# First attention of a four-part layer chain: q and k of a head from one product, their lines transposed once, rows moved between partitions by on-chip transfers

## The chip, the core and the metric

The kernel runs on one core of one Trainium2 chip. Its engines are PE (matrix products, with weight loads shown apart as PEld), DVE (vector), ACT (scalar, activations), POOL (general) and SP, which only issues transfers here. The metric is the device time of one execution in microseconds (us). Three runs of the kernel before took 2008.51, 2015.03 and 2027.37 us; the median is 2015.03.

## The reference, cut to what matters

A chain of four parts works on x of shape 8 x 512 x 256 (batch, token, feature). The change touches only the first, an attention with 16 heads of 16 features, whose logits get a bias from six-component lines:

```python
q, k, v = split((x @ w_qkv.T + b_qkv))                 # 16 heads of 16
std_logits = einsum('bhqd,bhkd->bhqk', q, k) * dh ** -0.5
write_lines = exterior(x_prev @ w1_write.T, x @ w2_write.T)   # 6 numbers per token and head, unit length
read_lines = exterior(x @ w1_read.T, x @ w2_read.T)
incidence = einsum('bqhp,bkhp->bhqk', read_lines, write_lines @ J6)
weights = sigmoid(decay_logits)[h] ** (q_pos - k_pos)  # for keys before the query, else 0
logits = std_logits + incidence * weights * bias_scale # masked above the diagonal
out = softmax(logits) @ v
```

`x` here is the output of a conditioning layer (itself a small attention), `J6` reverses the six components with two signs, and `x_prev` is x one token earlier. A mixture of experts, a second attention and a quantised product follow.

## The kernel before, in words

`stage_a1` computes the conditioning layer and the first attention. Everything is float32 apart from the row maxima, which work on bf16 copies.

The attention runs in 32 steps, one for each batch b (8) and head group g (4 groups of 4 heads). A group's four heads lie in four slots of 32 partitions. In a slot of a "table", partitions 0 to 15 hold q or k, and partitions 16 to 21 hold the lines. Tokens lie along the free axis (512, in four tiles of 128). A step works on two halves, A (heads 0 and 1 of the group) and B (heads 2 and 3). In each half:

- `incidence` (L694 on, product `sd`) multiplies the lines of `ktc` with those of `qt0` for the four diagonal tiles; `decay` (L706) multiplies by the decay weights on DVE; `scores` adds q times k and the negated row maxima `mt`; `weights` (L721) takes the exponential on ACT into `ed`, and POOL sets what is above the diagonal to zero (L722).
- `left` does the tiles left of the diagonal (products `o`), from `qts` (q and lines times the decay to the tile's edge) and `kts` (the same for keys); `left_weights` (L745) takes the exponential. Here the decay is folded into the tables, so one product over 32 rows gives score and bias. `kt1` is the first tile of `kts` times `far`, the decay over 128 tokens.
- `values` (`av`), `gather` (`av_t`) and, once a batch, `finish` (`ao_t`, `out_ps`, `xr`) produce the output. They trail by one step.
- `RowShift` computes the row maxima for the next step from bf16 copies `qb` and `kb` of `qt0` and `kts` (L621, L622): products `mx_d`, `mx_o`, `mx_m`, reductions on DVE, result `nm`, transposed as `nm_t` into `mt`.

`tables(b, g)` (L571) is a generator that prepares the tables three steps ahead. The loop advances it with `take(table)` at four places of a step and at its end:

1. at the end of a step: POOL writes the unit lines of q and k into two tiles `ln`, zero elsewhere (L581, 8 instructions)
2. at the head of the next step, after `nm_t`: `qt_ps` is the product of the padded weights `wqp` (32 columns a head, 16 of them zero) with `y`, two products of 128x512, and onto it four products of a lines tile with the identity, which turns the lines; ACT makes `qt0` of it (L596), POOL `qts` (L599)
3. after the row maxima of half A: `kt_ps` in the same way from `wkp`; DVE makes `kts` of it (L604), ACT `ktc`, only the rows of the lines (L607)
4. after the exponentials of half A: ACT makes one tile of `qts` and `kt1` with `far` (L609, L610)

Between these, `places(b, g)` (L968) lists what else is done at nine places of a step: the conditioning layer of batches b+2 and b+3 (class `Cond`: `spread` to `T` and `Tb`, `largest` with `ks_b`, `weights` with `ks_f`, `out` with `ko_ps`, `divided`, which writes `on` to memory; `back` loads it again as `oT`, and `result` with `y_ps` makes `y`), and `points(b+1)` (`vl_ps`, `pts`, `nrm`), which makes values and lines of the next batch.

Orders: all products of PE are pinned in the order in which the program writes them (L86 to L90). `in_order` (L1096) does the same for DVE, ACT and POOL over the whole stage. SP issues its transfers in one queue. PSUM has two banks for `mm` tiles (`nm_t`, tables, `vl_ps`, `av_t` and so on), four for `mx`, `o`, `ks` and `av`, two for `sd`. Order of a step around the change:

```python
together(h.incidence(A), last.left(B, 0) if last else ())
h.decay(A)
if last:
    last.left_weights(B, 0)
    h.mt = shift.turned()
place(0)
shift = RowShift((g + 1) % 4, tabs[steps[i + 1]]) if i + 1 < len(steps) else None
take(table)
place(1)
if shift:
    shift.first(A)
take(table)
place(2)
```

Of the kernel before, what the change touches and what calls it, by code (L numbers as in the profile page):

```python
# [19 lines left out]
P = 128  # L20
# [13 lines left out]
def rows(ap, n):  # L34

    return ap.rearrange("(c p) f -> p c f", p=P)
# [9 lines left out]
def tile_kernel(ctx: ExitStack, tc: tile.TileContext, t, out):  # L46
# [39 lines left out]
    def pmm(*a, **kw):  # L86
        pin(nc.tensor.matmul(*a, **kw))  # L87
# [48 lines left out]
    def stage_a1(ctx):  # L136
# [268 lines left out]
        wqp = load(xp, "wqp", [P, 2, 512], rows(t["wqp"], 2))  # L405
        wkp = load(xp, "wkp", [P, 2, 512], rows(t["wkp"], 2))
        bqp = load(xp, "bqp", [P, 4])
        bkp = load(xp, "bkp", [P, 4])
# [6 lines left out]
        nc.vector.tensor_scalar(bqp, bqp, DH ** -0.5, None, ALU.mult)  # L415
# [25 lines left out]
        isline = by_row("isline", [(16, 22, 1.0)])  # L441
        sgn = by_row("sgn", [(16, 22, 1.0), (17, 18, -1.0), (20, 21, -1.0)])
        isq = by_row("isq", [(0, 16, DH ** -0.5)])
        fq = xp.tile([P, 4, P], F32, tag="fq", name="fq")
        fk = xp.tile([P, 4, P], F32, tag="fk", name="fk")
        sq = cp.tile([P, 4], F32, tag="sq", name="sq")
# [13 lines left out]
        def decays():  # L460

            lnd = ln_sigmoid("lnd", dl, H)
            lnp = ln_sigmoid("lnp", dlp, 4)

            nc.vector.tensor_scalar(sq, bsp, sgn, isq, ALU.mult, ALU.add)

            nc.vector.tensor_scalar(lnp, lnp, isline, None, ALU.mult)
            for g in range(4):
                nc.scalar.activation(fq[:, g], ramp[:, 0], AF.Exp, scale=lnp[:, g:g + 1])
                nc.scalar.activation(fk[:, g], ramp[:, 1], AF.Exp, scale=lnp[:, g:g + 1])  # L470
            nc.scalar.activation(far, lnp, AF.Exp, scale=float(P))
            yield

            for h in range(H):
                nc.scalar.activation(wt[:, h], dif, AF.Exp, scale=lnd[:, h:h + 1])
                if h == 7:
                    yield
            nc.gpsimd.affine_select(wt, wt, pattern=[[0, H], [1, P]], compare_op=ALU.is_gt,
                                    fill=0.0, base=0, channel_multiplier=-1)
            yield  # L480


        lines = []
        for i in range(2):
            sl = xp.tile([P, NT, 4, 32], F32, tag=f"ln{i}", name=f"ln{i}")
            nc.gpsimd.memset(sl, 0.0)
            lines.append(sl)
# [83 lines left out]
        def tables(b, g):  # L571

            y = ys[b % 2]
            L, nrm = units[b]
            new = lambda nm, n=S: wk.tile([P, n], F32, tag=nm, name=nm, bufs=4 if nm in ("qts", "kts") else 3)
            gs = slice(g * P, (g + 1) * P)
            for sl, lo in ((lines[0], g * 4), (lines[1], H + g * 4)):
                hs = slice(lo, lo + 4)
                for j in range(NT):
                    l6 = L[:, j, hs]  # L580
                    nc.gpsimd.tensor_tensor(sl[:, j, :, 16:22], l6 if lo < H else rev6(l6),  # L581
                                            nrm[:, j, hs].unsqueeze(2).to_broadcast([P, 4, 6]), ALU.mult)
            yield
            qt0, qts, ktc, kts, kt1 = tabs[b, g] = \
                new("qt0"), new("qts"), new("ktc"), new("kts"), new("kt1", P)
            for w, q in ((wqp, True), (wkp, False)):
                sl = lines[0 if q else 1]
                ps = mm("qt_ps" if q else "kt_ps")
                for c in range(2):
                    pmm(ps, w[:, c, gs], y[:, c, 1:1 + S], start=c == 0, stop=False)  # L590

                for j in range(NT):
                    pmm(ps[:, j * P:(j + 1) * P], sl[:, j].rearrange("p h e -> p (h e)"), ident,
                        start=False, stop=j == NT - 1)
                if q:
                    nc.scalar.activation(qt0, ps, AF.Identity, bias=bqp[:, g:g + 1], scale=sq[:, g:g + 1])  # L596

                    for dst, src, n in ((0, 1, 2), (3, 3, 1)):
                        nc.gpsimd.tensor_tensor(  # L599
                            qts[:, dst * P:(dst + n) * P].rearrange("p (j q) -> p j q", q=P),  # L600
                            qt0[:, src * P:(src + n) * P].rearrange("p (j q) -> p j q", q=P),
                            fq[:, g].unsqueeze(1).to_broadcast([P, n, P]), ALU.mult)
                else:
                    nc.vector.scalar_tensor_tensor(  # L604
                        kts.rearrange("p (j k) -> p j k", k=P), ps.rearrange("p (j k) -> p j k", k=P),
                        bkp[:, g:g + 1], fk[:, g].unsqueeze(1).to_broadcast([P, NT, P]), ALU.add, ALU.mult)
                    nc.scalar.activation(ktc, ps, AF.Copy, scale=isline)  # L607
                yield
            nc.scalar.activation(qts[:, 2 * P:3 * P], qts[:, 3 * P:], AF.Copy, scale=far[:, g:g + 1])  # L609
            nc.scalar.activation(kt1, kts[:, 0:P], AF.Copy, scale=far[:, g:g + 1])  # L610
            yield
# [325 lines left out]
        take(point, 4)  # L937
        cond(2).load()
# [10 lines left out]
        table = tables(*steps[0])  # L949
        take(table, 4)  # L950
        state = states()
        shift = RowShift(0, tabs[steps[0]])
        table = tables(*steps[1])
        take(table)
        for gs in (A, B):
            shift.first(gs)
            shift.second(gs)
            take(table)
        shift.done()
        mt = shift.turned()  # L960
        take(table)
        table = tables(*steps[2])
        take(table)
# [4 lines left out]
        def places(b, g):  # L968
# [25 lines left out]
            elif g == 1:  # L994
                put(2, y, pt)
                put(3, y, pt)
                out[4].append(fin)
                out[5].append(fin)
# [5 lines left out]
            elif g == 2:  # L1004
# [3 lines left out]
                put(3, n, of_n("spread", 1))  # L1008
                put(4, n, of_n("out", 0, 0))
                put(5, n, of_n("divided", 0, 0))  # L1010
                out[5].append(fin)
                put(6, n, of_n("out", 0, 1))
                put(7, n, of_n("largest", 1))
                put(8, n, of_n("turned", 1), of_n("divided", 0, 1))
# [13 lines left out]
        for i, (b, g) in enumerate(steps):  # L1028
# [17 lines left out]
            shift = RowShift((g + 1) % 4, tabs[steps[i + 1]]) if i + 1 < len(steps) else None  # L1046
            take(table)
# [3 lines left out]
            take(table)  # L1051
# [5 lines left out]
            take(table)  # L1057
# [20 lines left out]
            if shift:  # L1078
                shift.second(B)
                shift.done()  # L1080
            for k in range(6, 9):
                place(k)
            table = tables(*steps[i + 3]) if i + 3 < len(steps) else none
            take(table)
# [833 lines left out]
def pack(i):  # L1918
# [15 lines left out]
    def slots(a):  # L1934

        o = np.zeros(a.shape[:-1] + (H, 32), np.float32)
        o[..., :DH] = a.reshape(a.shape[:-1] + (H, DH))
        return o.reshape(a.shape[:-1] + (H * 32,))
    d["wqp"], d["wkp"] = slots(w[:D].T), slots(w[D:2 * D].T)
    b = i[p + "b_qkv"]  # L1940
    d["bqp"], d["bkp"] = col(slots(b[:D])), col(slots(b[D:2 * D]))
# [64 lines left out]
```

## Time and profile before

| What | us |
|---|---|
| median of 3 runs | 2015.03 |
| profiled execution, own time | 2007.99 |
| its span in the trace | 2006.3 |
| PE busy in the span | 1830.6 |
| DVE busy | 1157.8 |
| ACT busy | 743.5 |
| POOL busy | 688.3 |
| the 32 attention steps, from about 170 to about 950 | 780 |

In the page, "busy" is the time in which an engine executes something. A group row gives the source line, the engine, the tiles written and read, the count, the busy time and the mean of one. L87 is the helper through which all products go, L90 the one for transposes, so products are told apart by tile name. In a float32 product each 128x512 operand pair shows as two records. An entry such as `[0.44 <-POOL ln L581]` means that the engine stood idle for 0.44 us before this row and that the named work ended the wait. SPq is the queue of SP: its times are those of issuing a transfer, not of moving data.

The largest groups of the tables, from the answers for their tiles: the 128x512 records of `qt_ps` and `kt_ps` 128 each with a median of 593 and 592 ns, the identity records 256 each at 275 ns; `qt0` 777 ns, `kts` 751 ns and `ktc` 687 ns, 32 of each.

### The profile page before, as it was taken

The page shows a single profiled execution, that of the slowest core. Times are in us where ns is not written, and L with a number is a line of the kernel's source. Part 1 is how long each engine was busy: PE and PEld are TensorE (multiplying, and loading weights), DVE is VectorE, ACT ScalarE, POOL GpSimd, SP SyncE. Part 2 cuts the span into 40 slices and gives each one's busy share as a digit, 9 for nine tenths or more (in the row PEclk, how much of TensorE's full clock was granted, in tenths as well). Part 3 has the DMA queues.
Part 4 walks back from the last instruction along what each step waited for, and adds up shares of the span by engine and source line. Part 5 has one row for each costly group of instructions (what it writes and reads, how often), then busy time and mean ns, then how long its engine had stood idle before and what let it go on. Part 6 is the DMA issues. An engine that isn't in the chain of part 4 may idle for free.

```text
span 2006.3 us, 46385 instructions
## 1 busy us (share of the span) xinstructions
PE 1830.6 (91%) x19658; PEld 1263.8 (63%) x19658; DVE 1157.8 (58%) x2646; ACT 743.5 (37%) x1444; POOL 688.3 (34%) x1071
## 2 busy tenths in 40 slices
PE   6789899999999998998788999999999889999997
PEld 3446566656656665655577888777777645555554
DVE  4445666656655656565579898622221256666666
ACT  3335444454444454443445445210110033333332
POOL 3324332433333333331387554000000244444422
PEclk7699998999899999987799999999999999999999
DMA  4110101111010102001364334222322211111100
GB/s 134 39 43 8 39 17 45 33 39 38 28 50 12 50 8 65 18 23 54 100 220 135 121 122 141 91 73 93 108 70 73 52 45 33 36 33 35 33 12 22
DMA packets 102108, 119.73 MB, mean 60 GB/s; under 512 B 45350, under 2 KB 82332, under 8 KB 101772
## 3 DMA queue, kind: packets, MB, share of 16 engines
q1 hardware_dynamic: 91660, 74.82, 12.3%
q0 software_dynamic: 10240, 41.95, 6.8%
q8 instruction: 154, 2.52, 0.5%
q14 instruction: 54, 0.44, 0.1%
HBM read 94.46 MB, written 22.27 MB: 58 GB/s over the span
## 4 chain that ended last, share of the span: by engine, by line
PE 64%; DVE 20%; ACT 5%; issue 4%; DMA 3%; POOL 3%; SPq 0%; DVEq 0%; POOLq 0%; ACTq 0%
PE y_ps L87 8%; PE h_ps L87 7%; PE sd L87 4%; PE qt_ps L87 3%; PE av L87 3%; PE vl_ps L87 3%; PE o L87 3%; PE kt_ps L87 2%; PE kx_ps L87 2%; PE k_ps L87 2%; PE qf_ps L87 2%; PE wo_ps L87 1%; PE kv_ps L87 1%; PE ks_f L87 1%; PE dsp L87 1%
## 5 line engine op out<-in xcount | busy, mean ns | idle before, releaser
L745 ACT ACTIVATE eo<-o 128x384 f32<-128x384 f32 x256 | 111.7, 488 | 234.9 <-PE o L87 227.7
L722 POOL TENSOR_SCALAR_AFFINE_SELECT ed<-ed 128x512 f32<-128x512 f32 x128 | 78.7, 637 | 309.6 <-ACT ed L721 309.6
L87 PE MATMUL h_ps<-bufT,w 128*128 128x320 f32 x512 | 141.8, 438 | 0.0
L87 PE MATMUL y_ps<-w,hT 128*128 128x256 f32 x640 | 139.4, 379 | 0.0
L87 PEld LDWEIGHTS y_ps<-w,hT 128*128 128x128 f32 x640 | 121.6, 190 | 17.4
L639 DVE TENSOR_REDUCE mx<-mx_d 128x4 f32<-128x512 f32 x128 | 82.0, 682 | 79.0 <-PE mx_d L87 79.0
L87 PEld LDWEIGHTS h_ps<-bufT,w 128*128 128x128 f32 x512 | 97.8, 192 | 43.7 <-DVE us L1560 3.4
L1532 ACT ACTIVATE hT<-h_ps,w_b 128x320 f32<-128x320 f32 x64 | 33.7, 527 | 245.7 <-PE h_ps L87 245.0
L1597 POOL MEMSET bn<- 128x512 f32 x1 | 0.5, 524 | 342.5 <-PE h_ps L87 342.5
L87 PE MATMUL hid_ps<-cat,wx 128*128 128x256 f32 x512 | 116.2, 380 | 0.0
L657 DVE TENSOR_REDUCE mx<-mx_m 128x3 f32<-128x384 f32 x128 | 65.3, 552 | 86.1 <-PE mx_m L87 86.1
L87 PEld LDWEIGHTS hid_ps<-cat,wx 128*128 128x128 f32 x512 | 96.4, 191 | 12.6
L87 PE MATMUL sd<-qt,ktc 32*128 32x128 f32 x1024 | 95.8, 321 | 7.8 <-ACT ed L721 7.0
L1534 DVE TENSOR_SCALAR hT<-h_ps,w_b 128x320 f32<-128x320 f32 x64 | 35.2, 551 | 114.8 <-PE h_ps L87 114.8
L706 DVE TENSOR_TENSOR sd<-sd,wt 128x512 f32<-128x512 f32 x128 | 82.3, 689 | 27.8 <-PE sd L87 23.0
L87 PEld LDWEIGHTS sd<-qt,ktc 32*128 32x128 f32 x1024 | 79.1, 217 | 27.0 <-ACT ed L721 11.8
L87 PE MATMUL o<-qts,kts 32*128 32x128 f32 (+1 forms) x768 | 94.4, 347 | 0.0
L1541 DVE TENSOR_TENSOR ye<-y_ps,bc_b 128x256 f32<-128x256 f32 x40 | 16.9, 423 | 107.4 <-PE y_ps L87 107.4
L87 PE MATMUL qt_ps<-y,w_wqp 128*128 128x512 f32 x128 | 76.3, 726 | 1.0 <-DVE z L349 1.0
L87 PEld LDWEIGHTS sd<-qt,kts 16*128 16x128 f32 x1024 | 71.0, 198 | 7.7 <-issue 6.1
L87 PEld LDWEIGHTS o<-qts,kts 32*128 32x128 f32 x768 | 74.8, 202 | 0.0
L87 PE MATMUL dsp<-o1h,xc 128*128 128x320 f32 x256 | 73.4, 439 | 1.2 <-DVE o1h L1313 1.2
(423 smaller groups left out, 4554.8 us busy)
## 6 DMA issues: line engine op xcount, KB each, us to landing
w<-in_W SPq DMA_DIRECT2D x16, 1024.0 KB
xT<-in_xT SPq DMA_DIRECT2D x8, 512.0 KB
kxd<-kxF SPq DMA_DIRECT2D x8, 512.0 KB
raw<-kxd SPq DMA_DIRECT2D x64, 64.0 KB
xr<-in_x SPq DMA_DIRECT2D x8, 512.0 KB
ond<-on SPq DMA_DIRECT2D x64, 64.0 KB
oT<-ond SPq DMA_DIRECT2D x8, 512.0 KB
x1d<-xr SPq DMA_DIRECT2D x8, 512.0 KB
```

What stands on the lines that cost most here:

```text
L87: pin(nc.tensor.matmul(*a, **kw))
L639: nc.vector.tensor_reduce(mx[:, g, 0:4], d[g].rearrange("p (j k) -> p j k", k=P), AX.X, ALU.max)
L657: nc.vector.tensor_reduce(mx[:, g, 5:14:4], o[g][:, :3 * P].rearrange("p (j k) -> p j k", k=P), AX.X, ALU.max)
L706: nc.vector.tensor_tensor(d3, d3, wt[:, self.hg * 4 + g].unsqueeze(1).to_broadcast([P, NT, P]), ALU.mult)
L722: zeroed.append(nc.gpsimd.affine_select(e, e, pattern=[[0, NT], [1, P]], compare_op=ALU.is_ge, fill=0.0, base=0, channel_multiplier=-1))
L745: nc.scalar.activation(e, self.o[g][:, :3 * P], AF.Exp)
L1532: nc.scalar.activation(dst, ps, AF.Relu, bias=b1[:, e, hc:hc + 1])
L1534: nc.vector.tensor_scalar(dst, ps, b1[:, e, hc:hc + 1], 0.0, ALU.add, ALU.max)
L1541: nc.vector.tensor_tensor(ye[:n], ps[:n], b2[:n, e * D:(e + 1) * D], ALU.add)
L1597: nc.gpsimd.memset(bn8, -0.125)
```

## The change

- The weights of q and k are interleaved by head into one array `wqk`: per head 16 columns of q and 16 of k. One product `qk_ps` (two 128x512) gives q in partitions 0 to 15 and k in 16 to 31 of a slot. Its ACT copy `qt0` carries both, with bias and scale (`sqk`).
- The lines of q and k go into one tile `lines`, those of q at 16 to 21 and those of k at 0 to 5 of a slot, and are turned by four PE transposes into `ln_t`. ACT copies it scaled into `lnT[:, 0]` (signs and bias scale for the lines of q), DVE times the decay into `lnT[:, 1]`.
- Twelve transfers per table on SP's queue, each from partitions to partitions of the on-chip memory, put the rows in place: k from `qt0` to `kts` (4), the lines of k to `ktc` and `kts` (4), the lines of q into `qt0` over k (4). `ktc` and `kts` of a table are the halves of one of four lasting tiles.
- The generator becomes a class `Table` with the parts `lines`, `turned`, `decayed`, `project`, `moved`, `scaled`. The loop places them apart: `lines` at a step's end, `turned` after `nm_t`, `decayed`, `project` and `moved` after the row maxima of half A, `scaled` (`qts`, `kt1` and the `far` copies) after those of half B.
- `RowShift` of the step after next, with its copies `qb` and `kb`, is now made at a step's end, not at the head of the step.
- Three calls in `places` move: the parts of `finish` from places 4 and 5 of g = 1 to 3 and 4, and from place 5 of g = 2 to 3; `turned(1)` of the conditioning layer (`Vt_ps`) from place 8 of g = 2 to 5.

```diff
-        wqp = load(xp, "wqp", [P, 2, 512], rows(t["wqp"], 2))
-        wkp = load(xp, "wkp", [P, 2, 512], rows(t["wkp"], 2))
+        wqk = load(xp, "wqk", [P, 2, 512], rows(t["wqk"], 2))
...
+        ktabs = []
+        for i in range(4):
+            kt = cp.tile([P, 2, S], F32, tag=f"kt{i}", name=f"kt{i}")
+            nc.gpsimd.memset(kt[:, 0], 0.0)
+            ktabs.append(kt)
...
+        class Table:
...
+            def lines(self):
...
+                for at, lo in ((16, g * 4), (0, H + g * 4)):
+                    hs = slice(lo, lo + 4)
+                    for j in range(NT):
+                        l6 = L[:, j, hs]
+                        nc.gpsimd.tensor_tensor(lines[:, j, :, at:at + 6], rev6(l6) if at == 0 else l6,
+                                                nrm[:, j, hs].unsqueeze(2).to_broadcast([P, 4, 6]), ALU.mult)
+            def turned(self):
+                ps = self.ps = mm("ln_t")
                 for j in range(NT):
+                    ptr(ps[:, j * P:(j + 1) * P], lines[:, j].rearrange("p h e -> p (h e)"), ident)
+                self.ln = wk.tile([P, 2, S], F32, tag="lnT", name="lnT", bufs=1)
+                nc.scalar.activation(self.ln[:, 0], ps, AF.Copy, scale=sln[:, self.g:self.g + 1])
+            def decayed(self):
+                nc.vector.tensor_tensor(
+                    self.ln[:, 1].rearrange("p (j k) -> p j k", k=P), self.ps.rearrange("p (j k) -> p j k", k=P),
+                    fk[:, self.g].unsqueeze(1).to_broadcast([P, NT, P]), ALU.mult)
+            def project(self):
...
+                    pmm(ps, wqk[:, c, g * P:(g + 1) * P], y[:, c, 1:1 + S], start=c == 0, stop=c == 1)
+                q = self.q = wk.tile([P, S], F32, tag="qt0", name="qt0", bufs=3)
+                nc.scalar.activation(q, ps, AF.Identity, bias=bqk[:, g:g + 1], scale=sqk)
+                for j in range(4):
+                    nc.sync.dma_start(out=self.kt[32 * j:32 * j + 16, 1], in_=q[32 * j + 16:32 * j + 32])
+            def moved(self):
+                ln, kt, q = self.ln, self.kt, self.q
+                for j in range(4):
+                    nc.sync.dma_start(out=kt[32 * j + 16:32 * j + 32], in_=ln[32 * j:32 * j + 16])
+                for j in range(4):
+                    nc.sync.dma_start(out=q[32 * j + 16:32 * j + 32], in_=ln[32 * j + 16:32 * j + 32, 0])
+            def scaled(self):
...
+                for dst, src, n in ((0, 1, 2), (3, 3, 1)):
+                    nc.gpsimd.tensor_tensor(
...
+                nc.scalar.activation(kt1, kts[:, 0:P], AF.Copy, scale=far[:, g:g + 1])
+                nc.scalar.activation(qts[:, 2 * P:3 * P], qts[:, 3 * P:], AF.Copy, scale=far[:, g:g + 1])
...
             elif g == 1:
                 put(2, y, pt)
                 put(3, y, pt)
+                out[3].append(fin)
                 out[4].append(fin)
-                out[5].append(fin)
...
                 put(3, n, of_n("spread", 1))
+                out[3].append(fin)
                 put(4, n, of_n("out", 0, 0))
-                put(5, n, of_n("divided", 0, 0))
-                out[5].append(fin)
+                put(5, n, of_n("divided", 0, 0), of_n("turned", 1))
                 put(6, n, of_n("out", 0, 1))
                 put(7, n, of_n("largest", 1))
-                put(8, n, of_n("turned", 1), of_n("divided", 0, 1))
+                put(8, n, of_n("divided", 0, 1))
...
             place(0)
-            shift = RowShift((g + 1) % 4, tabs[steps[i + 1]]) if i + 1 < len(steps) else None
-            take(table)
+            shift = ahead
+            if table:
+                table.turned()
             place(1)
             if shift:
                 shift.first(A)
-            take(table)
+            if table:
+                table.decayed()
+                table.project()
+                table.moved()
             place(2)
...
             if shift:
                 shift.second(B)
                 shift.done()
+            if table:
+                table.scaled()
             for k in range(6, 9):
                 place(k)
-            table = tables(*steps[i + 3]) if i + 3 < len(steps) else none
-            take(table)
+            ahead = RowShift((g + 2) % 4, tabs[steps[i + 2]]) if i + 2 < len(steps) else None
+            table = Table(*steps[i + 3]) if i + 3 < len(steps) else None
+            if table:
+                table.lines()
```

## The prediction

> **What bounds the kernel now.** I first read the stretch with the 32 attention steps (170 to 950 us, about 24.4 us each), then two halves of one step, then the order of time on each engine around the tables of two steps (b = 3, g = 3 into g = 0 into g = 1), and last who waits for whom. A step is (batch b, head group g); A and B are its halves, two heads each.
>
> ```profile
> 170.00:950.00 780.00, 721.06 (x11115) 475.55 (x11114) 478.09 (x937) 352.70 (x709) 282.43 (x552) 0.92 0.11 33
> 515.40:533.20 17.80, 17.30 (x365) 11.55 (x363) 7.41 (x13) 11.56 (x22) 8.93 (x17) 0.97 0.01 3
> 533.20:547.40 14.20, 12.05 (x225) 9.21 (x224) 12.48 (x27) 3.68 (x8) 1.84 (x3) 0.76 0.24 77
> ```
>
> The columns are window, length, busy us of PE, PEld, DVE, ACT, POOL, then granted clock, DMA share, GB/s. PE is busy 92% of the stage, but not everywhere is it the bound: half A of g = 2 (second row) is PE's, half B (third row) is VectorE's (12.48 of 14.20 us), and there PE idles and the granted clock falls to 0.76.
>
> ```profile
> 571.81 0.40 PE L90 MATMUL nm_t<-identb,nm 128*128 128x128 bf16 x4 [0.55 <-DVE nm L664]
> 572.40 1.99 PE L87 MATMUL qt_ps<-y,w_wqp 128*128 128x512 f32 x4 [0.20 <-DVE z L349]
> 574.83 1.16 PE L87 MATMUL qt_ps<-ident,ln 128*128 128x128 f32 x8 [0.44 <-POOL ln L581]
> 576.84 1.99 PE L87 MATMUL kt_ps<-y,w_wkp 128*128 128x512 f32 x4
> 578.66 1.05 PE L87 MATMUL kt_ps<-ident,ln 128*128 128x128 f32 x8
> 581.96 1.96 PE L87 MATMUL y_ps<-oT,wo 128*128 128x512 f32 x4 [0.86 <-DMA oT<-ond]
> ...
> 573.98 0.61 POOL L361 COPY on<-z 128x512 f32<-128x512 f32 x1 [2.69 <-DVE z L360]
> 574.55 1.51 POOL L581 TENSOR_TENSOR ln<-L,nrm 128x24 f32<-128x24 f32 x8
> ...
> 574.61 1.78 SPq L366 DMA_DIRECT2D ond<-on  x4
> 578.24 0.38 SPq L371 DMA_DIRECT2D oT<-ond  x1
> ```
>
> This is the head of a g = 0 step. The lines (L581) are ready only at 576.06; PE hides that behind the q product and waits 0.44 us. The load of oT (L371) goes out when the stores of on have landed, and its result is used 3.72 us after the issue.
>
> ```profile
> 595.86 1.07 ACT L285 COPY T<-raw 128x1024 f32<-128x1024 f32 x1
> ...
> 595.64 1.26 POOL L722 TENSOR_SCALAR_AFFINE_SELECT ed<-ed 128x512 f32<-128x512 f32 x2 [11.87 <-ACT ed L721]
> 597.00 1.04 POOL L286 CAST Tb<-T 128x1024 bf16<-128x1024 f32 x1
> 598.00 1.51 POOL L581 TENSOR_TENSOR ln<-L,nrm 128x24 f32<-128x24 f32 x8
> ...
> 597.46 0.40 PE L90 MATMUL nm_t<-identb,nm 128*128 128x128 bf16 x4
> 597.70 1.94 PE L87 MATMUL qt_ps<-y,w_wqp 128*128 128x512 f32 x4
> ...
> 507.09 0.66 PE L90 MATMUL av_t<-ident,avs 128*128 128x128 f32 x4 [0.75 <-DVE xr L800]
> ```
>
> The head of g = 1: mask (L722), T on ACT, Tb and lines on POOL form one chain, again covered by the q product. The last row is one of the 12 waits of av_t for xr, 15.9 us in the list of waits of the stage and PE's largest there.
>
> **The change, part by part.** *PE work.* From start to next start, q's table takes 2.8 us and k's 2.8 (597.70 to 600.36, 601.38 to 604.09, a little over 2.7 each): 5.6. After: one product, 1.9, and four transposes. Four by-identity blocks cost 1.05; four transposes cost 0.66 by the row of av_t. The Trainium skill (TensorE: Matmul & The Clock Gate, Terms) has the transpose mode four times as fast for FP32, which would be 0.26, an estimate; the row decides[...]. So 1.9 + 0.6 = 2.5, 3.1 to 3.2 us less in each of 29 steps with a table, about -92 us if PE were the bound all the time; by the page's rule -104.
>
> *What PE waits for instead.* The lines were the last of PE's table work and had 1.9 us of product ahead of them. Now the transposes come straight after nm_t and the product comes after the row maxima. Besides, qts (L599, 1.14 us on POOL) and the two copies by far (0.3 each, ACT) move from half A to the end of half B, between the mask and the lines, and qb and kb (0.52 each, ACT) to the step's end. ACT and POOL work in the traced order, so what stands behind them waits: step by step,
> - g = 0: lines at 576.06 as before (they wait for on, which waits for DVE's z). PE stands from 572.2 to about 575.5; transposes to 576.3, maxima (1.2) to 577.5, product to 579.4, where before k's table ended at 579.65. The gain is gone. The copy of q ends at 580.2. In the built order of SP three of the four moves kt<-q stand ahead of oT; at 0.3 us each (rows of 8x256 copies, 0.27 to 0.30; the 64 KB raw rows have 0.44) oT is issued at 581.2, not 578.24, and y_ps starts at 585 instead of 581.96. Cost: +2.8 us.
> - g = 1: the mask ends 596.9, qts 598.0, far 598.3, T 599.3, Tb 600.4, lines 601.9. Transposes end at 602.2 where q's table ended at 600.36. The product ends at 605.3; vl_ps takes its PSUM bank and waits for the copy of q: 606.2 against 604.09, +2.1. ao_t, moved ahead of av, waits 0.5 for pts. out_ps (2.0 us) moves from half B to A, which removes the wait of av_t (0.75) and 0.74 of DVE work from half B, where DVE is the bound; at its end the table load for nrm now waits for far, so eo comes late, and g = 2 wins only 2.0 back. Together +2.6.
> - g = 2 and 3: half A of g = 2 carries the other out_ps (+2.0, of which 0.3 fills a wait: +1.7). From incidence(B) on, DVE loses 0.71 of xr and about 1.3 of waits, lines come 1.9 earlier, MT no longer stands behind qb, kb and qt, and C and the product are done together: ks_f starts 3.2 earlier. Together -1.5.
>
> Sum: 7 x 2.8 + 7 x 2.6 - 6 x 1.5 = +29. Three steps late in the stage (871, 897, 926 us) have no such chain: -2.5 each. The start of the stage waits twice for moves, hidden by the maxima of the first step (118.9 to 129.3): +2. That makes **+23 us**.
>
> *The moves.* Twelve a table, 384 in all, 16 partitions of 2 or 4 KB. The Trainium skill (DMA: Bandwidth & Descriptors, Anatomy of one DMA) gives a fixed 2.0 us per DMA plus bytes over 436 GB/s, measured on the other issue path; paid one after another, an estimate, that is 12 x 2.1 = 25 us a table, where about 12 us lie between the copy of q and its use at the end of half B: +13 us x 29. Here four stores of 64 KB are issued in 1.78 us and have landed 2.2 us after the last: they overlap. So 12 x 0.3 + 2.2, about 6 us (7.5 by the raw rows); hidden. Their cover is half B; without it, kt1 on ACT stops, and behind it far, qb, kb and the next step's eo. DVE's new multiply costs what kts did (0.75), ACT's two copies what qt and ktc did (0.78 + 0.69). Eight waits ahead of that multiply: 0.02 to 0.18 each by the semaphore rows of SP, at most 1.4, in a gap of 2.4 us: nothing. kxd, raw and x1d stand behind moves by up to 4 us and are used a step later: nothing.
>
> *The clock.* The row 533.20 shows 0.76 where PE idles 2.15 us. The Trainium skill (TensorE: Matmul & The Clock Gate, Part 1: The HAM clock gate) says PE drops to half speed after an idle window of about 3.4 us and returns after a busy one. This speaks against the change: its stalls before the transposes (3.3 us in g = 0, 3.8 in g = 1, about 4 in g = 3) and before y_ps (3.8) end in PE-bound halves, while the stalls it removes lay in DVE's. One window at half speed loses 1.7 us. No clock effect: +0; all four with two windows: 7 x 4 x 3.4 = +95. A stall of such a length need not fill a free-running window, so I count two of four with one window: 7 x 2 x 1.7 = **+24**.
>
> Total +47 on the profiled execution's 2007.99 us (span 2006.3), 2055. That execution lies 7 us under the median of 2015.03, against which the next runs stand: **2062**.
>
> **Rivals.** *Faster.* PE's saving survives: if the lines are there when PE asks and oT is not late, g = 0 and g = 1 win about 3 each, g = 2 and 3 as above: -7.5 x 7 = -52, and the late steps, -60 in all: 1955. It decides at the wait before the transposes: below 3.1 us in g = 0 and g = 1 the step gains. For it speaks PE's 92%; against it that L581 ends at 576.06 and 599.5 before even with qts out of its way. *No change.* The stalls are as summed but the clock holds and POOL is a little ahead: 2015 to 2038. *Moves on the path.* If a move takes its place in line alone, kt1 waits every step: 13 x 29 = +380, 2390; if only the last few land late, +2 a step, 2120. The overlapping stores speak against it.
>
> **How the numbers follow.** Forecast (stalls, some clock) 0.63; moves on the path in part 0.07; no change 0.18; faster 0.12. One per cent is 20 us, about what a measurement of this kernel can tell. So slower by over 1% 0.70, within 0.18, faster 0.12. The range: from 2000, which leaves out the faster case, to 2120 (+23 + 80 of clock, or moves landing 2 us late).
>
> **What would show it.** Right: idle of PE before ln_t ended by POOL's lines, 3 us or more in g = 0 and 1; y_ps waiting for oT some 4 us; av_t's wait for xr gone; about 92 us less PE busy; granted clock in the stage below 0.92. Wrong: ln_t without a wait (faster), or ACT's kt1 waiting for DMA (much slower).

## The result, and the profile after

The changed kernel takes 2134.68 us (median of 4 runs, 2133.3 to 2137.55), the kernel before beside it 2017.16. The ratio is 1.0582, with a 95% interval of 1.053 to 1.0635: about 117 us slower. The forecast was slower, 2062; the time lies above its range, which ended at 2120.

The page of the changed kernel, its engine row and two rows of its 40 slices (tenths busy, tenths of clock), and last the clock row of the kernel before:

```profile
PE 1834.0 (86%) x19113; PEld 1227.5 (58%) x19146; DVE 1160.6 (54%) x2652; ACT 737.2 (35%) x1438; POOL 691.8 (32%) x1074
...
PE   6768788797887878888876899999999989999997
...
PEclk7668787787887878887777999999999999999999
...
PEclk7699998999899999987799999999999999999999
```

PE has 545 records fewer than before, and yet as many busy microseconds (1830.6 before): work was taken away, and what is left runs slower. The clock rows say why. The clock is lower in the first 22 slices, which reach to the end of the attention's stage, and as before after them. In the windows of the changed kernel (window, length, busy us of PE, PEld, DVE, ACT, POOL, granted clock, DMA share, GB/s) the stage and two of its steps read:

```profile
170.00:1080.00 910.00, 747.81 (x10932) 458.60 (x10960) 494.04 (x954) 358.26 (x725) 291.35 (x564) 0.79 0.18 44
...
643.70:678.40 34.70, 25.25 (x239) 13.96 (x240) 16.01 (x32) 9.35 (x20) 9.64 (x20) 0.75 0.21 56
...
678.40:713.70 35.30, 28.60 (x324) 17.77 (x324) 18.77 (x36) 15.31 (x31) 13.10 (x24) 0.84 0.12 23
```

Clock 0.79 in the stage; before it was 0.92 in the prediction's window and 0.91 up to the end of the stage. The two steps are g = 0 and g = 1 of one batch; before they took 25.7 and 28.5 us.

PE's list of waits in the stage (total, times, longest), and the start of that g = 0 step in order of time, PE and then SP's queue:

```profile
PE ln_t L90 <- POOL lines L589: 47.9, 23, 4.1
PE y_ps L87 <- DMA oT<-ond: 34.9, 6, 5.8
PE ln_t L90 <- ACT eo L768: 18.1, 5, 3.6
...
PE vl_ps L87 <- ACT qt L610: 6.1, 7, 0.9
```

```profile
643.76 0.40 PE L90 MATMUL nm_t<-identb,nm 128*128 128x128 bf16 x4 [1.26 <-DVE nm L687]
...
647.52 1.11 PE L90 MATMUL ln_t<-ident,lines 128*128 128x128 f32 x4 [3.36 <-POOL lines L589]
...
650.27 3.78 PE L87 MATMUL qk_ps<-y,w_wqk 128*128 128x512 f32 x4
661.37 3.52 PE L87 MATMUL y_ps<-oT,wo 128*128 128x512 f32 x4 [5.81 <-DMA oT<-ond]
667.12 1.98 PE L87 MATMUL y_ps<-oT,wo 128*128 128x512 f32 x4
...
646.57 1.79 SPq L366 DMA_DIRECT2D ond<-on  x4
654.90 1.78 SPq L612 DMA_DIRECT2D kt<-qt  x3
656.86 0.44 SPq L371 DMA_DIRECT2D oT<-ond  x1
657.35 0.51 SPq L612 DMA_DIRECT2D kt<-qt  x1
657.90 2.54 SPq L617 DMA_DIRECT2D kt<-lnT  x4
660.55 2.43 SPq L619 DMA_DIRECT2D qt<-lnT  x4
```

Read it as a chain. The lines come 3.36 us late. The same four records of a 128x512 product pair take 3.78 us after that wait and 1.98 at 667.12: PE runs at half speed. So q's copy is later by 1.8 us, with it the three moves in SP's queue (0.59 us each to issue), the load of oT behind them, and y_ps, which waits 5.81 us, and then runs at half speed itself (3.52). One stall makes the next.

Step lengths from `nm_t` to `nm_t`, mean of batches 1 to 5, in us, and the time at half speed between 170 us and 10 us behind the last `nm_t`, added up from the trace's clock records (two kernels of the experiments stand here already; "mean stretch" is the mean length of an unbroken time at half speed):

| | g = 0 | g = 1 | g = 2 | g = 3 | batch | at half speed | mean stretch |
|---|---|---|---|---|---|---|---|
| before | 26.0 | 28.6 | 32.3 | 25.1 | 112.0 | 143 | 6.5 |
| after | 34.7 | 35.7 | 32.4 | 27.5 | 130.3 | 385 | 10.2 |
| e1b_fill | 31.5 | 33.6 | 30.2 | 25.9 | 121.3 | 205 | 7.1 |
| c1 | 28.3 | 26.0 | 32.7 | 26.5 | 113.4 | 232 | 5.8 |

The prediction's 24.4 us a step comes from a window without the first and the last steps; from the first `nm_t` to the last (132.0 to 983.5 us) an interval takes 27.5 us.

A batch is 18.3 us longer, the seventh 14.6. The start of the stage has a further 16 (first `nm_t` 5.1 later, first batch 11.0 longer). The last three step intervals give 17.1 back, and the work behind them takes 23.1 more. These two belong together. In the kernel before, the first rows xh of the next part (the mixture of experts) are made among the last attention steps, 31.7 us ahead of the last `nm_t`; in the changed kernel they are made 30.2 us behind its last `nm_t`, and PE waits for what is made of them (first row before, the others after):

```profile
951.87 2.08 ACT L1331 ACTIVATE xh<-xres,nmr,rs 128x256 f32<-128x256 f32 x4 [2.98 <-DVE nmr L1343]
...
1118.38 2.07 ACT L1367 ACTIVATE xh<-xres,nmr,rs 128x256 f32<-128x256 f32 x4 [0.44 <-DVE nmr L1379]
...
1136.77 0.69 PE L90 MATMUL cat_t<-ident,hh 128*128 128x128 f32 x2 [13.96 <-DVE hh L1398]
```

The longest such wait was 4.5 us before. The program of that part is the same in both kernels, but every version with the change has these rows late (27 to 30 us behind the last `nm_t`). No run moved them back, so what set their order stays open.

### The profile page after: what moved, and what is told of

Read it like the earlier page. It is cut to its first block, busy times and chain, and to the rows that moved or that the text cites. A ratio compares the mean times of both kernels' runs of the same rounds, so it can differ in the third digit from the quotient of the medians.

```text
span 2134.0 us, 46325 instructions
## 1 busy us (share of the span) xinstructions
PE 1834.0 (86%) x19113; PEld 1227.5 (58%) x19146; DVE 1160.6 (54%) x2652; ACT 737.2 (35%) x1438; POOL 691.8 (32%) x1074
## 4 chain that ended last, share of the span: by engine, by line
PE 60%; DVE 22%; ACT 6%; issue 4%; DMA 3%; POOL 3%; SPq 1%; ACTq 0%; POOLq 0%; DVEq 0%
PE y_ps L87 8%; PE h_ps L87 7%; PE qk_ps L87 5%; PE av L87 4%; PE vl_ps L87 3%; PE sd L87 3%; PE mx_d L87 2%; PE o L87 2%; PE kx_ps L87 2%; PE qf_ps L87 2%; PE out_ps L87 2%; PE kv_ps L87 1%; PE dsp L87 1%; PE k_ps L87 1%; DMA oT<-ond 1%
## 5 line engine op out<-in xcount | busy, mean ns | idle before, releaser
L87 PE MATMUL sd<-qt,kt 32*128 32x128 f32 (+1 forms) x2048 | 173.1, 305 | 8.6 <-ACT ed L744 6.7
L87 PEld LDWEIGHTS sd<-qt,kt 32*128 32x128 f32 (+1 forms) x2048 | 150.2, 208 | 42.7 <-issue 25.4
L87 PE MATMUL o<-qts,kt 32*128 32x256 f32 (+1 forms) x1024 | 130.9, 371 | 0.0
L87 PE MATMUL qk_ps<-y,w_wqk 128*128 128x512 f32 x128 | 113.3, 1038 | 0.2 <-ACT mt L696 0.2
L90 PE MATMUL ln_t<-ident,lines 128*128 128x128 f32 x128 | 35.3, 428 | 86.4 <-POOL lines L589 64.9
L87 PEld LDWEIGHTS o<-qts,kt 32*128 32x128 f32 x1024 | 94.0, 204 | 0.0
L90 PEld LDWEIGHTS ln_t<-ident,lines 128*128 128x128 f32 x128 | 23.0, 179 | 94.4 <-POOL lines L589 93.9
```

The source lines that it names most:

```text
L90: pin(nc.tensor.transpose(*a))
```

## The experiments

Theory 1: the waits are about as forecast, and most of the rest is PE's clock. Theory 2: the twelve moves a table are the loss. Theory 3: the order of work on POOL and ACT. Times are given as ratios to the kernel before on the same chip, with 95% intervals; the changed kernel has 1.0582.

**Keep PE busy in its waits (e1_fill, e1b_fill).** Products of the constant tile `above` go into a bank that the next real product clears (tables 2 and 3 of a batch are made in steps g = 0 and g = 1):

```diff
                 ps = mm("y_ps")
+                if b and oc == 0:
+                    for _ in range(18):
+                        pmm(ps, identb, above, start=True, stop=True)
...
                 ps = self.ps = mm("ln_t")
+                if self.g in (2, 3):
+                    for _ in range(14):
+                        pmm(ps, identb, above, start=True, stop=True)
```

> The changed kernel, with products without use put where PE stands idle: 14 (128x512, bf16) into the bank of ln_t ahead of its transposes in the steps g = 0 and g = 1, and 18 into the bank of y_ps ahead of its first product; at 0.22 us each at full clock that is 3.1 and 3.9 us. What is computed stays the same. No wait is taken away; only PE is kept busy in it. Theory 1 (the stalls are as predicted, and most of the loss is PE's clock, which they bring down to half in halves that PE bounds): half-speed time falls from 580 us to under 400, time 2040 to 2080. Theory 2 (the twelve moves, by their issue on SP and their traffic, are the loss) and theory 3 (the order of the work on POOL and ACT, with waits longer than summed; the clock only follows): 2130 to 2160, no gain.

Measured: 1.0535 (1.051 to 1.056), a gain that the intervals leave open, and half-speed time of the whole run 433 us (581 without). In the steps g = 2 and g = 3, without filler, the clock is down already at `nm_t` (0.61 us where 0.40 is full speed), and waits of 1.3 and 2.1 us ahead of the transposes are still there; in g = 2:

```profile
695.29 0.61 PE L90 MATMUL nm_t<-identb,nm 128*128 128x128 bf16 x4
...
697.18 1.11 PE L90 MATMUL ln_t<-ident,lines 128*128 128x128 f32 x4 [1.28 <-POOL lines L592]
```

So filler went into all four steps (14, 9, 7, 11 products, and 24 at y_ps):

> As the first kernel with filler, but in all four steps of a batch (14, 9, 7 and 11 products without use ahead of the transposes in g = 0, 1, 2, 3, and 24 ahead of the first y_ps), since that run still had 433 us at half speed, most of it begun by the wait of 1.3 to 2.1 us in g = 2 and g = 3. Theory 1 (clock): half-speed time below 330 us, ratio to the kernel before 1.035 to 1.045 (1.0535 with filler in two steps). Theory 3 (the waits and the order themselves are the loss, clock a small part): half-speed time falls as much, but the ratio stays at 1.048 to 1.056.

Measured: 1.0315 (1.0277 to 1.0353), half-speed time 376. Added work on PE makes the kernel 54 us faster, give or take 13: 1.0582 less 1.0315, times the 2003 us of before. In all four steps of the table above the length falls, by 1.6 to 3.2 us. The half-speed time did not fall as far as theory 1 said, the time fell further. Half-speed time in the first 12 us of a step, mean of batches 1 to 5 (us), shows where it fell:

| | g = 0 | g = 1 | g = 2 | g = 3 |
|---|---|---|---|---|
| before | 0.9 | 0.0 | 1.5 | 0.2 |
| after | 9.5 | 6.9 | 8.7 | 10.5 |
| e1_fill | 1.4 | 0.7 | 9.3 | 9.5 |
| e1b_fill | 3.7 | 2.0 | 2.1 | 2.9 |

The last two kernels differ in filler alone. So in g = 2 and g = 3, where the clock fell at the end of the step before, work in a short wait brings it back, and without that work it stays down.

Theory 1 holds for about half of the loss at least. 63 us are left, and part of them is filler that overran: in e1b_fill the transposes start 4.4 us a batch later than in the changed kernel, which is at most 28 us over the 26 tables with filler. The filler in a g = 0 step:

```profile
610.26 0.61 PE L90 MATMUL nm_t<-identb,nm 128*128 128x128 bf16 x4 [0.33 <-DVE nm L693]
...
611.66 4.23 PE L87 MATMUL ln_t<-above,identb 128*128 128x512 bf16 x12 [0.22 <-issue]
615.73 0.60 PE L90 MATMUL ln_t<-ident,lines 128*128 128x128 f32 x4
617.18 1.99 PE L87 MATMUL qk_ps<-y,w_wqk 128*128 128x512 f32 x4
620.48 5.35 PE L87 MATMUL y_ps<-above,identb 128*128 128x512 bf16 x23
627.30 1.96 PE L87 MATMUL y_ps<-oT,wo 128*128 128x512 f32 x4 [1.48 <-DMA oT<-ond]
```

qk_ps takes 1.99 us instead of 3.78. But in the mean of batches 1 to 5 y_ps still starts 16.04 us after `nm_t` (17.45 without filler, 10.44 before the change). So 1.4 of the 7.0 us by which it is late came from the clock, and the late oT is mostly something else.

**Moves and oT (e2_ot, e7_nomove, e2c_ot, e8_both).** e2_ot holds the four moves from q to kt behind the load of oT by an order without a wait; e2c_ot does it for all twelve. e7_nomove has no moves, and e8_both has none and the filler of e1b_fill; both leave out the rows that the moves bring.

```diff
-                nc.sync.dma_start(out=self.oT, in_=rows(self.ond, 2))
+                loaded.append(nc.sync.dma_start(out=self.oT, in_=rows(self.ond, 2)))
...
+        def move(dst, src):
+            ins = nc.sync.dma_start(out=dst, in_=src)
+            if loaded:
+                tc.add_manual_dep(ins.ins, loaded[-1].ins.name, ...)
```

> The changed kernel, with the load of oT held ahead of the four moves from q to kt in SP's queue. Theory 1: the wait of y_ps falls from about 5.8 us to about 4 in seven steps (-13) with a little clock behind it: 2105 to 2130. Theory 2: the queue is the loss: below 2090. Theory 3: 2115 to 2135.

> The changed kernel without its twelve moves a table; it leaves out the rows that they bring (keys and the lines of q and k stay zero or hold other rows), all other work stays. Theory 1: it is little better than the kernel with oT ahead, 2100 to 2125, since the waits before ln_t stay. Theory 2: the whole loss is gone, 2000 to 2050. Theory 3: 2105 to 2135.

> The changed kernel, with all twelve moves of a table held behind the load of oT (in the run with oT ahead of the moves from q alone, two moves of lines, which wait for lnT, still stood ahead of it). If SP's order is what the moves cost, the wait of y_ps falls from 5.8 to about 2 us, step g = 0 from 34.6 to about 29, and the ratio comes near to that without moves (1.032): 1.035 to 1.042. If the moves cost by their traffic or by the ends that kt1, qts and the copies wait for, it stays above 1.048.

> The changed kernel with filler in all four steps and without its twelve moves (it leaves out the rows that they bring). Filler alone gave 1.0315, no moves alone 1.0317, each some 26 thousandths less than 1.058. If clock and moves were two separate losses, they add: 1.005. If the moves lose mostly by the clock that y_ps's wait brings down, the two overlap: 1.015 to 1.025. What is left then is the order of POOL and ACT and the filler's own time.

| | ratio | interval |
|---|---|---|
| e2_ot | 1.0562 | 1.0537 to 1.0587 |
| e7_nomove | 1.0317 | 1.0293 to 1.0341 |
| e2c_ot | 1.0388 | 1.0366 to 1.041 |
| e8_both | 1.0249 | 1.0225 to 1.0272 |

The first brought nothing that can be told from none: y_ps still waited up to 3.5 us, because two moves of lines stood ahead of oT and waited for lnT, which held up all behind them: oT was issued 10.5 us after `nm_t`. e7_nomove lies between what theories 1 and 2 said. With all moves behind oT it is issued after 6.4 us:

```profile
503.86 1.80 SPq L366 DMA_DIRECT2D ond<-on  x4
507.47 0.38 SPq L371 DMA_DIRECT2D oT<-ond  x1
512.20 3.11 SPq L491 DMA_DIRECT2D kt<-qt  x4
...
512.82 1.98 PE L87 MATMUL y_ps<-oT,wo 128*128 128x512 f32 x4
```

oT goes out as soon as the stores of on have landed, y_ps has no wait, and g = 0 takes 27.2 us instead of 34.7, just as without any moves (27.2). So in g = 0 the moves' whole price, 7.5 us, was their place ahead of oT, with the clock that followed it; over a batch e2c_ot wins 6.9 us of the 8.2 that e7_nomove wins. Without moves 14 us more are gone, most of them at the start of the stage: the first `nm_t` comes 7.1 us earlier and the first batch is 5.2 shorter. In the steady steps theory 2 holds for the place, not for traffic or for waits of kt1. Filler and no moves overlap (1.0249, not 1.005), but this says little of the clock: the 24 products ahead of y_ps stay in e8_both, where they cover no wait, and y_ps starts 14.8 us after `nm_t` instead of 11.7 in e7_nomove.

**Order of POOL and ACT (e4_late, e3_proj, e5_places).** e4_late makes qts, kt1 and the last tile of qts in half A of the next step:

```diff
             h.weights(A)
+            if made:
+                made.scaled()
...
-            if table:
-                table.scaled()
             for k in range(6, 9):
                 place(k)
```

> The changed kernel, with qts, kt1 and the last tile of qts made where the kernel before made them, after the exponentials of half A of the next step, so that POOL goes from the mask to the lines directly. Theory 1: the wait before ln_t in g = 1 falls from 3.6 to about 2 us, and its clock with it: -7 x 1.5 and as much again or twice that for the clock, 2090 to 2115. Theory 2: no gain, 2130 to 2150. Theory 3: it is the main part of the loss, below 2070.

Measured: 1.0432 (1.0383 to 1.0482), some 30 us less, as theory 1 said: the lines of g = 1 are ready 2.1 us after `nm_t`, not 4.5. e3_proj puts the product ahead of the transposes, as a cover for the lines:

```diff
             if table:
+                table.project()
                 table.turned()
...
                 table.decayed()
-                table.project()
                 table.moved()
```

> The changed kernel, with the product of q and k (qk_ps) moved ahead of the transposes of the lines, so that it covers their wait as the q product did before; the copy of q and the moves come earlier too. Theory 3: about 2 us less wait before ln_t in each step and the wait of vl_ps for q (0.9) gone: 27 x 2 + 7 x 0.9 = -60, ratio about 1.028 (1.058 for the changed kernel). Theory 1: the same and as much again from the clock: 1.00 to 1.015. Theory 2 (moves): oT is still behind moves, ratio 1.045 to 1.055.

Measured: 1.0283 (1.0246 to 1.032). One moved line gives back 60 us, what theory 3 said, without the clock's share that theory 1 added: half-speed time is still 451 us. e5_places is the kernel before with only the change's other places for finish and Vt_ps:

```diff
             elif g == 1:
+                out[3].append(fin)
                 out[4].append(fin)
-                out[5].append(fin)
```

> The kernel before with one part of the change alone: finish one place earlier (ao_t, out_ps ahead of av, in half A of g = 1 and g = 2) and Vt_ps from the end of g = 2 to its middle. The tables stay as before. From the traces: half A of g = 1 +2.0 to +2.5, half B, which is DVE's, -0.4 to -1.1, g = 2 between -1 and +1: 7 x (0 to 2.5), ratio 1.00 to 1.009. In the sum on record this part counted about +1.5 a batch in g = 1 and g = 2 together.

Measured: 1.0044 (1.0027 to 1.0062), 9 us slower. This part removes a wait and loses.

**Together (e6b_all, c1, c2).** e6b_all is e3_proj, e4_late and the order of e2_ot; c1 has the order of e2c_ot instead, and finish and Vt_ps where the kernel before has them.

> The changed kernel with three parts together: the product ahead of the transposes, qts and the copies by far back in half A of the next step, and oT held ahead of the moves from q to kt. Theory 3: the gains add (60 + 30 + 4): ratio about 1.01. Theory 1: the clock comes back as well, half-speed time below 350 us: 0.98 to 1.00. Theory 2: the moves still cost their 50 us (1.0569 to 1.0317 without them): not below 1.02.

> Product ahead of the transposes, qts and the copies by far back in half A of the next step, all moves behind oT, and the places of finish and Vt_ps as before the change: what is left of the change is its table work and its moves. From the parts: 1.0218 less 0.0044 for the places, less 3 us in seven steps for oT with its clock (0.010 to 0.02): 0.995 to 1.010. Below 0.99 would mean that PE's saving (3 us a step) is coming through.

Measured: e6b_all 1.0218 (1.0176 to 1.0259), so the gains overlap; c1 1.0031 (1.0011 to 1.005). In c1 a g = 0 step begins:

```profile
583.00 0.40 PE L90 MATMUL nm_t<-identb,nm 128*128 128x128 bf16 x4 [0.56 <-DVE nm L696]
583.60 1.99 PE L87 MATMUL qk_ps<-y,w_wqk 128*128 128x512 f32 x4 [0.20 <-DVE z L349]
586.76 0.88 PE L90 MATMUL ln_t<-ident,lines 128*128 128x128 f32 x4 [1.18 <-POOL lines L596]
...
593.51 3.63 PE L87 MATMUL y_ps<-oT,wo 128*128 128x512 f32 x4 [2.41 <-DMA oT<-ond]
```

Two short waits, and still y_ps at half speed. c2 is c1 with filler at such waits (11 products at y_ps, 6 at ks_f, 5 at ln_t in g = 0, 3 and 8 at av_t):

> The kernel of the last run (product first, late qts, moves behind oT, places as before the change; 1.0031) with filler at its remaining waits: 11 products ahead of the first y_ps (it waited 2.4 us), 6 ahead of ks_f (1.3), 5 ahead of the transposes in g = 0 (1.2), 3 and 8 ahead of av_t in g = 1 and g = 2 (0.75, 2.1). If the clock is what still holds PE's saving back, half-speed time falls from 397 us to below 330 and the ratio to 0.985 to 0.997. If the rest is DVE's and the chains of waits, the filler only takes its place: 1.000 to 1.010.

Measured: 0.9972 (0.9948 to 0.9997), just above the range that was to show the clock, with half-speed time at 253 us. This is the best version, and by its interval barely faster than the kernel before. Of PE's 3 us a step, a batch (110.0) keeps 2.0 us in all.

**A stall alone (b_stall, b_stall_fill), and a control (b_fill).** In the kernel before, POOL writes the lines three times over in 13 tables; the second run puts 14 filler products ahead of their q product; the third has filler only at the waits that the kernel before has anyway.

```diff
+            late = g in (2, 3) and 2 < b * 4 + g < 28
-            for sl, lo in ((lines[0], g * 4), (lines[1], H + g * 4)):
+            for sl, lo in ((lines[0], g * 4), (lines[1], H + g * 4)) * (3 if late else 1):
```

> The kernel before, with POOL writing the lines three times over (same values) for the tables made in g = 0 and g = 1, 13 tables: they come 3.0 us later, so that PE stands about 3 us ahead of the identity blocks of qt_ps, where it stood 0.44 or less. Nothing else is changed. If a stall costs only its own length, 13 x 3.0 = 39, ratio 1.015 to 1.021. If it also brings the clock down in the half that follows (1.7 to 3.4 us lost each), 13 x 4.7 to 6.4 = 61 to 83: 1.029 to 1.043, with 90 us or more of added half-speed time.

> The same late lines in the kernel before, with 14 products without use (3.1 us) ahead of the q product in those tables, so that PE works while it waits. If the clock is part of the price of a stall: half-speed time back near 280 us and a ratio of 1.015 to 1.021, below that of the stall without filler by 1 to 2 per cent. If not: the same ratio as without filler or up to 0.5 per cent more.

> A control: the kernel before with filler at its own waits (4 products ahead of the first y_ps, 3 and 8 ahead of av_t in g = 1 and g = 2, where it waits 0.75 to 2.3 us for xr). If filler helps any kernel, 0.99. If it helps only where a stall ends in a half that PE bounds: 0.996 to 1.004.

Measured: 1.0158 (1.0123 to 1.0192), 1.018 (1.0145 to 1.0216), 1.0032 (1.0008 to 1.0057), with 281, 260 and 212 us at half speed (277 before). The wait of qt_ps for the lines rose from 3.5 to 30.4 us in the stage, and the time by about 32: over the whole kernel these stalls cost little more than their length, and filler gains nothing. By steps filler does two things that cancel. In g = 0, where the stall is 3.4 us, the step takes 27.9 us with it and 29.6 without. In g = 1, where the stall is 1.6 us, the 14 products overrun, and it takes 31.7 and 30.2. A g = 0 and a g = 1 step of b_stall:

```profile
595.91 1.57 PE L87 MATMUL qt_ps<-ident,ln 128*128 128x128 f32 x8 [3.40 <-POOL ln L582]
...
599.13 3.78 PE L87 MATMUL kt_ps<-y,w_wkp 128*128 128x512 f32 x4
...
605.37 1.98 PE L87 MATMUL y_ps<-oT,wo 128*128 128x512 f32 x4
...
624.68 1.16 PE L87 MATMUL qt_ps<-ident,ln 128*128 128x128 f32 x8 [1.61 <-POOL ln L582]
626.69 1.99 PE L87 MATMUL kt_ps<-y,w_wkp 128*128 128x512 f32 x4
```

After 3.40 us of idleness one product pair runs at half speed, 1.8 us lost, and then PE works without a gap and is back at full speed; after 1.61 us nothing is lost. The forecast's 1.7 us a window is right for a single stall, and filler gives just that back in g = 0. What the changed kernel has is another thing: wait upon wait, so that its half-speed stretches last 10.2 us, not 6.5. In the control filler at the waits of the kernel before wins nothing.

## Why the prediction was right about the side and wrong about the size

- *PE's saving is lost in waits for lines and oT:* right. The waits ahead of the transposes are 3.4 us in g = 0, ended by POOL's lines, and 3.6 in g = 1, where the profile names ACT's eo, though the transposes start 0.5 us ahead of the end of the lines in both steps. In g = 3 the wait was 2.2 us, not about 4, and g = 2 had one of 1.3. y_ps waits 5.8 us for oT, where about 4 were forecast. The waits of av_t for xr are gone, as forecast.
- *g = 0, +2.8:* too small. At nearly full clock (e1b_fill) it is +5.5 (+8.8 in the changed kernel). The lines came where the forecast had them, 4.25 us after `nm_t`. The misses are behind: a move takes 0.59 us to issue, not 0.3 (the raw rows' 0.44 was nearer), y_ps starts 4.4 us after the issue of oT, not 3.7, and about 1.4 of the 5.5 is filler that overran. e2c_ot shows that the order in SP's queue was the thing to price: without it in the way g = 0 is only 1.2 longer than before.
- *g = 1 to g = 3, +2.6 and -1.5:* +1.1 forecast, +3.7 at nearly full clock (+5.0, -2.1, +0.8 in e1b_fill, filler that overran in it), +9.6 in the changed kernel. For g = 1 the windows of its halves in e1_fill, whose half A has full clock, answer to those of the kernel before (first e1_fill, then before):

```profile
661.61:682.53 20.92, 17.74 (x162) 10.65 (x160) 7.09 (x13) 9.02 (x18) 8.99 (x19) 1.00 0.20 39
682.53:695.29 12.76, 11.60 (x179) 7.44 (x179) 11.73 (x23) 6.34 (x13) 4.03 (x6) 0.75 0.01 2
```

```profile
597.46:612.88 15.42, 15.42 (x156) 10.11 (x154) 6.83 (x12) 7.33 (x16) 6.66 (x16) 1.00 0.08 19
612.88:625.99 13.11, 11.95 (x187) 8.29 (x187) 11.39 (x23) 6.02 (x12) 5.45 (x7) 0.87 0.01 3
```

  Half A is 5.5 longer: 2.9 to the start of vl_ps (2.1 forecast; 1.2 of the 2.9 is filler that overran, as the transposes start 5.25 us after `nm_t`, not 4.01), 0.5 for ao_t and 2.0 for out_ps, both as forecast. Half B, from which out_ps and xr were taken, wins 0.35, because DVE stays its bound (11.73 us of 12.76).
- *Moves hidden:* right for half B, where no waits of kt1 for moves add up. Wrong for the start of the stage, forecast at +2: 16 us, of which the run without moves takes away 8.5.
- *The clock, +24:* this is the step that failed. The term counted two of the four long stalls of a batch, with one window each, and gave nothing to the rest. In batches 1 to 5 the changed kernel is at half speed for 52.6 us a batch, the kernel before for 13.7: 11 windows of 3.41 us more, not two. Most of them, 33 us, lie in the first 12 us of the four steps, g = 2 and g = 3 with their short waits included; another 7.5 lie around y_ps in g = 0, and are gone in e2c_ot and e7_nomove. Filler (22.6 us a batch) gives 54 us back, its own time already paid, and up to 82 if all of its overrun is added. The price of one lone stall was right, as b_stall shows. What was left out is that a wait too short to count holds the clock down once it is down, and that work at half speed makes the next wait longer. On the average a window cost less than the forecast's 1.7 us: filler takes away 30 us at half speed and 9.0 us of time a batch, about 1.0 us for each 3.41, its overrun not taken off.
- *Waits, +23:* between 35 and 63 us, by the same two bounds, the places (9) included. This term was too small as well: the move's time to issue and the order in SP's queue, and the start of the stage.
- *92 us less busy PE:* wrong as put; fewer records at half speed are as long.

Rivals: *faster* fell, since the wait before the transposes was above 3.1 us in g = 0 and g = 1; *no change* fell; *moves on the path* was true at one point of a steady batch only, by their place in SP's queue and not by their landing, and at the start of the stage.

The Trainium skill (TensorE: Matmul & The Clock Gate, Terms) puts the penalty of throttling at about the throttled time times a half. By that the 304 us more at half speed would be an estimate of 152 us, more than the whole loss of 117. Filler took 205 us of half-speed time away, by the page an estimate of 102; the time fell by 54 (82 at most), and in b_fill 64 us less at half speed brought nothing. In these runs time at half speed cost less than its half on the average, and nothing at the waits of the kernel before.

What stays open: how the loss divides exactly between waits and clock, as filler overran and the single gains overlap (60 for e3_proj, 30 for e4_late, 39 for e2c_ot, 9 for the places, yet 110 together in c1). And why a kernel with 3 us less PE work a step ends level even in c2. A part shows in its trace. Its last `nm_t` comes 23.8 us earlier than in the kernel before, and the work behind it takes 21.5 us more: the experts' first rows are late there too (28.5 us behind the last `nm_t`), cat_t waits 6.5 us for ss and 13.6 for hh, and 7.3 us are lost in stages that the change does not touch. Inside the batches its waits of av_t for xr (16.4 us) and DVE's half B point to DVE, but no run took work from DVE.

## What to carry to other kernels

A product that the change makes smaller may have been the cover of a slow producer: look at what stands between the producer's end and its first use, and keep the cover (here one moved call, 60 us). Price each stall once for its length, and ask whether PE then works without a gap; if another wait follows within some microseconds, count the clock for the whole stretch, and count a short wait (1.3 us here) wherever the clock is down already. A transfer's own landing may be hidden and its place in the queue may not: whatever waits in front of an urgent load holds it up.

## What the runs showed of the hardware

The clock changes in steps of 3.41 us in the records. With PE's busy share worked out from the trace for each such window of the changed kernel's stage, the window ahead of a fall has PE busy 61% in the median (67% in the kernel before), and three quarters of these windows lie between 12% and 73%: a window need not be idle for a fall. The window ahead of a return is busy 100% in the median, and above 96% in nine of ten; windows at half speed that are followed by another have 73%. The Trainium skill (TensorE: Matmul & The Clock Gate, Part 1: The HAM clock gate) speaks of an idle and a busy window; for the return the runs agree, for the fall it was enough that PE stood idle for a third of it. So PE busy for three quarters of a window at half speed did not bring the clock back; at full speed a tenth of the windows that are followed by another are below 86%. One rival to the waits is not separated: over eleven of these traces, of the windows at half speed with PE busy over 96%, the clock came back behind 81% of those without transposes (233 of 288) and behind 36% of those with transposes for 30% or more (30 of 84), and the change put transposes at the head of the step. Filler brought the clock back with the same transposes in place.

A move of 16 partitions within the chip's memory takes SP 0.54 us to issue from q and 0.59 us from lnT (medians of 128 and 256), where the load of oT takes 0.38 in the kernel before and 0.44 among the moves.
